# Four graph layers on one core: the set-up in one new order, and layer 1's second filter product ahead of the nodes' products

## The chip, the cores and the metric

The kernel runs on one core of a Trainium2 chip. A core has five engines with a queue of instructions each: TensorE (PE, matrix products, with weight loads counted apart as PEld), VectorE (DVE), ScalarE (ACT), GpSimd (POOL) and SyncE (SP, which here only issues DMAs). ACT and POOL issue DMAs too. Each engine works through its own queue in order. The metric is the device time of one execution in microseconds (us).

## The reference

128 graphs of 64 nodes with 128 channels each, `x [128, 64, 128]`, and `adj [128, 64, 64]`, which is zero for about three quarters of the entries and else a number from 0.05 to 6. Four layers follow one another, each as `x = layernorm(x + layer(x, adj))`. Cut to what matters here:

```python
# layer 0: 20 gaussians of the distance, only edges below 5 count
f = exp(coeff * adj[..., None] ** 2)
rcut = 0.5 * (cos(adj * pi / 5) + 1) * (adj < 5)
W = (ssp(f @ fw1 + fb1) @ fw2 + fb2) * rcut[..., None]
agg = einsum('bjf,bijf->bif', x @ w_in2f, W)
out = ssp(agg @ ow1 + ob1) @ ow2 + ob2
# layer 1: the same with 64 gaussians, and W * adj * adj
g = exp(coeff1 * (adj[..., None] - offsets) ** 2)
Wf = (ssp(g @ W1.T + b1) @ W2.T + b2) * adj[..., None]
y = einsum('bjf,bijf->bif', x @ Wa.T, Wf * adj[..., None])
out = ssp(y @ Wd1.T + bd1) @ Wd2.T + bd2
# layer 2: graph convolutions with the normalised (adj + 1) and elu
# layer 3: relu((normalised (adj + 1) @ x) @ W.T + b)
```

`ssp(v)` is `log(1 + exp(v)) - log 2`. In layers 0 and 1 a filter is computed for every edge: first product (gaussians by W1), exp and log, second product, and then a sum over the neighbours of each node.

## The kernel before

The work is done in `sparse_stack`. (A dense version exists behind a flag and does not run with these inputs.) Two graphs form a pair, so there are 64 pairs with 128 nodes on the 128 partitions.

**Set-up.** Only the edges that exist are computed. To pack them tightly, each graph's nodes are ranked by their number of neighbours, so that nodes with about the same number share a row of slots. The steps, by their names in the code:

- `entries` takes the adjacency, graphs on the partitions, in four quarters. For each quarter DVE writes `within` (below the cutoff) and `some` (not zero).
- `count` adds up each of them over the neighbours, in halving steps. This gives `degree` and `close`. The key of a node is made of both.
- The graphs are sorted by their total (`keys`, `place_on`, `graph_to`); POOL scatters `adj_sorted` and `x_sorted` in that order.
- `rank(0)` ranks the nodes of each graph: four large comparisons `before`, and a count.
- `permuted(0)` permutes the rows of the first eight pairs with PE: 0/1 matrices `there` from DVE, 16 products into `permuted`, a copy to `rows` by ACT, a write to `perm0` and a read back as `ad`. The later eighths go by indirect DMAs on POOL (`scatter`) and loads on SP.
- `compact(0)` takes the nearest neighbours of each row in rounds of eight (`comb`, `at`), and `pack` writes the distances `dc`, the neighbours `jc` and the weight `w` (a Sin on ACT, squared) to DRAM (`store`).
- `loads(n)` reads d, j and w of a pair back, spread over the partitions; in layer 0 the d of one pair comes in six loads.
- `rank(1)` ranks a second time for the later use of the slots, piece by piece. In before, `gathering` runs it, and its pieces lie between those of the compaction.
- A single number of the zero filter (`zero_filter`) is computed by a few small steps of ACT and PE.

The weights of layers 0 and 1 (`filter_layer`) and of layers 2 and 3 are loaded by ACT's queue, all of them ahead of the set-up's first large ACT steps, `below` and `rows`.

**The loop.** It visits 128 pairs, 64 for layer 0 and 64 for layer 1, in three chunks k = 0, 1, 2 each. Three chunks are in flight: c starts, c1 follows, c2 ends.

- `filter_in(c)`: the first product `px` (line 1774), then `h` = exp on ACT. `gather(c1)`: the features of the neighbours by a 0/1 matrix `hot`, product `pg` (line 1800), copied to `g` by ACT. `softplus(c)`: the log on ACT.
- `filter_out(c2)`: the second product `pw` (line 1788). `message(c2)`: DVE's `m` = (pw + bias) * g (line 1814). After a pair's third chunk `slot_sums` reduces m into `agg` in DVE steps that lie in the queue `sums`.
- Work on nodes lies in further queues of generators, of which each slot of the loop runs one step: `befores` (transposing x and multiplying with the input weights), `nodes` (the products after the sum, and the layernorm), `convs` (layer 2 and 3), and `last` for the last small groups. Where a step ends with a product, `owing` lets the step that reads it come one slot later. A full group is four pairs.

`px`, `pg` and `pw` have one PSUM buffer each (two banks), the node products two (`ps_n`).

**The order.** `in_order` chains the instructions of an engine as they are written. In before it does so for DVE and POOL in the set-up, and for all five engines from the loop on; PE, ACT and SP are placed by the scheduler in the set-up, so that a load that waits for nothing may go out earlier than where it is written.

Of the kernel before, what the change touches and what calls it, by code (L numbers as in the profile page):

```python
# [12 lines left out]
F32 = mybir.dt.float32  # L13
# [588 lines left out]
def sparse_stack(ctx: ExitStack, tc: tile.TileContext, t: dict, out: bass.AP, flag):  # L602
# [122 lines left out]

    def load_matrix(name, rows=C):
        w = const.tile([rows, C], F32, name=f"w_{name}")
        nc.scalar.dma_start(w, t[name])
        return w
# [4 lines left out]
    def load_column(name):  # L734
        b = const.tile([P, 1], F32, name=f"c_{name}")
        nc.scalar.dma_start(b, column(name))
        return b
# [19 lines left out]
    def load_rows(name):  # L757
        b = const.tile([P, C], F32, name=f"b_{name}")
        nc.scalar.dma_start(b, dram_ap(t[name], 0, [[0, P], [1, C]]))
        return b  # L760
# [18 lines left out]


# [96 lines left out]
    with (  # L877
        tc.tile_pool(name="count", bufs=2) as pre,
        tc.tile_pool(name="count_ps", bufs=1, space=PSUM) as ps_pre,
    ):  # L880
        entries = pre.tile([NB, A, A], F32, name="entries", bufs=1)
        some = pre.tile([NB, A, A], BF16, name="some", bufs=1)
        within = pre.tile([NB, A, A], BF16, name="within", bufs=1)
        for q in range(4):
            cut = slice(16 * q, 16 * (q + 1))
            nc.sync.dma_start(entries[:, cut, :], adj[:, cut, :])
            nc.vector.tensor_scalar(within[:, cut, :], entries[:, cut, :], CUTOFF, None, ALU.is_lt)
            nc.vector.tensor_scalar(some[:, cut, :], entries[:, cut, :], 0.0, None, ALU.is_gt)

        for into, at in x_parts:  # L890
            nc.sync.dma_start(into, x_flat[:, at])

        degree, close = given[:, 0, :], given[:, 1, :]
        run(deque([count(some, pre, degree), count(within, pre, close)]), -1)
        nc.vector.scalar_tensor_tensor(close, close, -float(A), degree, ALU.add, ALU.add)

        total = const.tile([NB, 1], F32, name="total")
        nc.vector.tensor_reduce(total, given[:, 0:2, :], AX.XY, ALU.add)
        nc.vector.tensor_scalar(total, total, key_of[:, 0:1], key_of[:, 1:2], ALU.mult, ALU.add)
        keys = pre.tile([P, P], F32, name="keys", bufs=1)  # L900
        nc.vector.tensor_scalar(keys, ident, total, None, ALU.mult)
        keys_ps = ps_pre.tile([P, P], F32, name="keys_ps")
        nc.tensor.matmul(keys_ps, lhsT=all_ones, rhs=keys, start=True, stop=True)
        ranking = deque([rank(0, close, pre)])
        run(ranking, 16)
        nc.vector.tensor_scalar(keys, keys_ps, total, None, ALU.is_gt)
        nc.vector.tensor_reduce(total, keys, AX.X, ALU.add)
        nc.vector.tensor_scalar(place_on, columns, total, None, ALU.is_equal)
        to = const.tile([NB, 1], U32, name="graph_to")
        nc.vector.tensor_copy(to, total)  # L910
        nc.gpsimd.indirect_dma_start(
            out=adj_sorted.rearrange("g i j -> g (i j)"),
            out_offset=bass.IndirectOffsetOnAxis(ap=to, axis=0),
            in_=entries.rearrange("g i j -> g (i j)"), in_offset=None,
        )
        run(ranking, -1)
        nc.vector.tensor_mul(width0, width0, width0)
        nc.vector.reciprocal(coeff0, width0)
        nc.vector.tensor_scalar(coeff0, coeff0, -0.5, None, ALU.mult)
        nc.vector.tensor_scalar(neg_off[0], neg_off[0], -1.0, None, ALU.mult)  # L920

        below = pre.tile([NB, A * A], BF16, name="below", bufs=1)
        nc.scalar.activation(
            below, entries.rearrange("g i j -> g (i j)"), AF.Relu, scale=-1.0, accum_out=odd[:, 0:1]
        )

    work = ctx.enter_context(tc.tile_pool(name="swork", bufs=2))
    node = ctx.enter_context(tc.tile_pool(name="snode", bufs=2))
    ps_x = ctx.enter_context(tc.tile_pool(name="sps_x", bufs=1, space=PSUM))
    ps_g = ctx.enter_context(tc.tile_pool(name="sps_g", bufs=1, space=PSUM))  # L930
    ps_w = ctx.enter_context(tc.tile_pool(name="sps_w", bufs=1, space=PSUM))


    compacting = ctx.enter_context(ExitStack())
    cpt = compacting.enter_context(tc.tile_pool(name="scompact", bufs=1))
# [18 lines left out]


# [15 lines left out]

    def goes_to(i):
        if i == 0:
            sorted_ = ps_n.tile([P, 512], F32, tag="n", name="sorted")[:, 0 : 3 * A]
            nc.tensor.matmul(
                sorted_, lhsT=place_on, rhs=given.rearrange("g k i -> g (k i)"),
                start=True, stop=True,
            )
        from_ = sorted_[:, 2 * A :] if i == 0 else places[1]
        nc.vector.tensor_scalar(codes[i], from_, row[:, 2:3], None, ALU.add)  # L980
        tp = ps_n.tile([P, 512], F32, tag="n", name=f"goes_t{i}")
        nc.tensor.transpose(tp[0:A, 0:P], rows_on if i else codes[0], ident)
        by_pair = tp[0:A, 0:P].rearrange("i (p b) -> i p b", b=2)
        for b in range(2):
            to = slice(b * A, (b + 1) * A)
            nc.vector.tensor_copy(a_all[to, :, A] if i else index[to, :], by_pair[:, :, b])

        code = const.tile([P, A], BF16, name=f"code_b{i}")
        nc.vector.tensor_copy(code, codes[i])
        nc.sync.dma_start(code_dram[i], code)  # L990
        if i == 0:
            nc.vector.tensor_copy(table.rearrange("g k i -> g (k i)"), sorted_[:, 0 : 2 * A])

    def find_rows():

        tp = ps_n.tile([P, 512], F32, tag="n", name="graphs")
        nc.tensor.matmul(tp[:, 0:P], lhsT=row_wide, rhs=place_on, start=True, stop=True)
        by_pair = tp[:, 0:P].rearrange("i (p b) -> i p b", b=2)
        row_f = spare[:, 5 * P : 5 * P + NP]
        for b in range(2):  # L1000
            half_ = slice(b * A, (b + 1) * A)
            nc.vector.tensor_scalar(
                row_f[half_], by_pair[half_, :, b], float(A), near[half_], ALU.mult, ALU.add
            )
        nc.vector.tensor_copy(at_row, row_f)


# [27 lines left out]
    def permuted(s, again=False):  # L1035
# [18 lines left out]
        if s == 0 and not again:  # L1054
            goes_first()
            flat = ps_x.tile([P, 2, 512], F32, tag="x", name="permuted0")[:, 0, :]
# [11 lines left out]
            )  # L1068
            for h, engine in enumerate((nc.sync, nc.scalar)):
                from_ = perm0.rearrange("k (q h r) j -> h (k q) r j", h=2, r=8)[h]  # L1070
                engine.dma_start(ad[64 * h : 64 * (h + 1), :, 0:A], from_)
        permuted_rows[s] = ad
        yield

# [5 lines left out]
    def pack(layer, s, d, j):  # L1080
# [28 lines left out]
        for r in range(8):  # L1109
            to = slice(bases[r], bases[r] + caps[r])  # L1110
            nc.gpsimd.tensor_copy(jc[:, to], j[:, r, 0 : caps[r]])
        store("j", jc)
        w = packed("w", F32)
        if layer == 0:
            def sine():
                act(w, dc, AF.Sin, bias=half_pi, scale=PI / (2 * CUTOFF))

            if s == 0:
                sine()
            else:  # L1120
                yield from wait_steps(6)
                sines.append(sine)
                while sines:
                    yield
            yield from wait_steps(PACE if s else 0)
            (nc.gpsimd if s else nc.vector).tensor_tensor(w, w, w, ALU.mult)
# [3 lines left out]
        stored.add((layer, s))  # L1130
        yield
# [148 lines left out]
    def loads(n, engine=nc.sync):  # L1280
        yield_, late = later_loads(n, engine)
        late()
        return yield_

    def later_loads(n, engine=nc.sync):
# [11 lines left out]
        def load(to, name, first, n):  # L1297

            (engine if name == "d" else nc.sync).dma_start(to, dram_ap(slots[layer, name][s], first, [[0, to.shape[0]], [1, n]]))  # L1299
# [3 lines left out]
        for b in range(2):  # L1303
            rows, first = slice(A * b, A * (b + 1)), at + b * size
            if layer == 1:
                load(d[rows], "d", first, size)
            else:
                for k, end in enumerate((NG0, 2 * NG0, A)):
                    load(d[A * b + NG0 * k : A * b + end], "d", first + k * third, third)

        def late():
            for b in range(2):
# [6 lines left out]

    def load_a(s):  # L1320

        a_pairs = (adj_sorted if s else adj).rearrange("(p b) i j -> (b i) p j", b=2)
        nc.sync.dma_start(a_all[:, part(s), 0:A], a_pairs[:, part(s), :])
# [10 lines left out]
    load_a(0)  # L1334
    nc.sync.dma_start(x_all[:, part(0), :], x_pairs[:, part(0), :])
    permuted_rows, goes, hots = {}, {}, {}
    side, again0, sines = deque(), [], deque()

    off1 = offsets1()
# [695 lines left out]
```

## Time and profile before

| | us |
|---|---|
| median of three runs | 1592.23 (1591.06 to 1595.87) |
| the profiled execution | 1607.39 |
| its span | 1605.5 |
| PE busy | 1432.6 |
| DVE busy | 1355.6 |
| ACT busy | 1335.6 |
| POOL busy | 732.5 |

The profile shows one execution, by a hardware profiler; "busy" is the time in which an engine worked on instructions. Its own time is 15.2 us above the median of the runs, so differences are better read from it than levels. The page's slices (40 of equal length) show PE busy under 80% in the first four and the last two, and at 90% or more in all between. The first product of the loop starts at 75.25 us; layer 0 ends and layer 1 starts about in the middle of the span, at 850 us layer 1 is under way, and from some 1540 us on only the last groups' node work is left.

### The profile page before, as it was taken

To read this page: it belongs to the slowest core of one execution; us is meant where nothing else is said; L and a number is where in the kernel's file an instruction comes from. 1 tells how busy PE (TensorE), PEld (TensorE's weight loads), DVE (VectorE), ACT (ScalarE), POOL (GpSimd) and SP (SyncE) were. 2 spreads that over 40 slices of the span, in tenths; PEclk is the share of its full clock that TensorE was granted. 3 is DMA by queue.
4 is the path that set the end of the run, shared out by engine and by line. 5 is a ranking of instruction groups with operands and counts; after the bars stand their busy time and mean duration, and the time that the engine had idled before them with its cause. 6 is when DMAs were issued, how large, how long until landed. Compare 5 with 4: busy or idle time off the path is not lost.

```text
span 1605.5 us, 24221 instructions
## 1 busy us (share of the span) xinstructions
PE 1432.6 (89%) x6813; PEld 802.6 (50%) x6813; DVE 1355.6 (84%) x3547; ACT 1335.6 (83%) x1847; POOL 732.5 (46%) x1174
## 2 busy tenths in 40 slices
PE   1276999999999999999999999999999999999974
PEld 1133454555554555555445555556555555555543
DVE  7687889999989999889878888888888888888873
ACT  1266898989888989889999998999989999899842
POOL 2425246555655644425611255433554435543454
PEclk9998999999999999999999999999999999999976
DMA  7654464645455544447555455544554455455200
GB/s 257 209 123 114 112 138 123 135 124 145 124 136 134 136 122 113 113 111 178 149 151 129 128 142 132 129 124 125 144 132 120 120 134 138 124 141 123 64 8 23
DMA packets 122289, 205.67 MB, mean 128 GB/s; under 512 B 47956, under 2 KB 80034, under 8 KB 121506
## 3 DMA queue, kind: packets, MB, share of 16 engines
q1 hardware_dynamic: 110784, 187.61, 46.7%
q0 software_dynamic: 6576, 14.99, 2.9%
q10 hardware_dynamic: 4786, 1.43, 0.4%
q8 instruction: 57, 0.93, 0.3%
q14 instruction: 86, 0.70, 0.2%
HBM read 185.29 MB, written 18.64 MB: 127 GB/s over the span
## 4 chain that ended last, share of the span: by engine, by line
PE 45%; DVE 27%; ACT 10%; DMA 7%; issue 6%; SPq 3%; POOL 2%; another core or an unknown queue 1%; ACTq 0%; DVEq 0%; POOLq 0%
PE pw L1788 16%; PE px L1774 9%; DVE m L1814 8%; PE pg L1800 7%; DVE agg L1837 6%; ACT h L951 4%; DVE hot L1762 2%; DVE at L1182 2%; PE hw L1673 2%; SPq L1299 2%; ACT g L951 2%; PE y L1453 2%; ACT d L951 1%; DVE st L1415 1%; PE o L1584 1%
## 5 line engine op out<-in xcount | busy, mean ns | idle before, releaser
L951 ACT ACTIVATE h<-h,half 128x672 f32<-128x672 f32 (+13 forms) x385 | 353.1, 917 | 0.1
L1837 DVE TENSOR_REDUCE agg<-m 128x16 f32<-128x240 f32 (+13 forms) x896 | 325.0, 411 | 3.0
L951 ACT ACTIVATE g<-pg 128x672 f32<-128x672 f32 (+12 forms) x384 | 303.2, 790 | 26.4 <-DVE m L1814 13.2
L1800 PE MATMUL pg<-hot,ys 64*128 64x336 f32 (+12 forms) x1536 | 308.8, 478 | 7.9 <-DVE hot L1762 7.0
L1788 PE MATMUL pw<-h,w_L_gnn_W2T 128*128 128x420 f32 (+5 forms) x768 | 301.9, 516 | 15.2 <-DVE m L1814 15.2
L1814 DVE SCALAR_TENSOR_TENSOR m<-pw,c_L_gnn_b,g 128x840 f32<-128x840 f32 (+5 forms) x192 | 200.9, 1046 | 115.6 <-PE pw L1788 88.0
L1788 PE MATMUL pw<-h,w_L_gnn_fw 128*128 128x336 f32 (+6 forms) x768 | 264.4, 467 | 28.3 <-DVE m L1814 22.0
L951 ACT ACTIVATE h<-px,c_L_gnn_b 128x840 f32<-128x840 f32 (+5 forms) x192 | 178.7, 931 | 53.6 <-PE px L1774 52.8
L1814 DVE SCALAR_TENSOR_TENSOR m<-pw,c_L_gnn_fb,g 128x672 f32<-128x672 f32 (+6 forms) x192 | 176.9, 921 | 50.0 <-PE pw L1788 31.2
L951 ACT ACTIVATE h<-px,c_L_gnn_fb 128x672 f32<-128x672 f32 (+6 forms) x192 | 159.3, 830 | 71.2 <-PE px L1774 46.4
L1788 PEld LDWEIGHTS pw<-h,w_L_gnn_W2T 128*128 128x128 f32 x768 | 132.5, 191 | 141.1 <-DVE m L1814 37.6
L1774 PE MATMUL px<-d,fw 64*128 64x336 f32 (+6 forms) x768 | 166.2, 507 | 40.8 <-DMA d<-d_dram 29.2
L1800 PEld LDWEIGHTS pg<-hot,ys 64*128 64x128 f32 x1536 | 146.3, 188 | 108.1 <-issue 17.5
L1788 PEld LDWEIGHTS pw<-h,w_L_gnn_fw 128*128 128x128 f32 x768 | 132.5, 191 | 120.6 <-DVE m L1814 62.2
L1762 DVE SCALAR_TENSOR_TENSOR hot<-j,row,w 128x1212 f32<-128x1212 bf16 (+12 forms) x128 | 177.0, 1383 | 9.0 <-issue 9.0
L1774 PE MATMUL px<-d,w1t 64*128 64x420 f32 (+5 forms) x768 | 181.1, 548 | 1.7 <-ACT h L951 1.6
L1422 POOL TENSOR_SCALAR rs<-mv 128x4 f32<-128x4 f32 x61 | 14.5, 237 | 344.0 <-DVE mv L1416 335.6
L1774 PEld LDWEIGHTS px<-d,fw 64*128 64x128 f32 x768 | 59.7, 188 | 132.2 <-ACT h L951 44.4
L951 ACT ACTIVATE d<-d,neg_off 128x1212 f32<-128x1212 f32 (+12 forms) x128 | 119.8, 936 | 7.1 <-issue 7.1
L1428 POOL TENSOR_SCALAR x_all<-ny,mv,rs 128x128 f32<-128x128 f32 x124 | 116.4, 947 | 3.3
L1030 POOL DMA_INDIRECT rows<-comb,goes x64 | 67.9, 1061 | 97.1 <-DMA rows<-comb,goes 69.6
L1774 PEld LDWEIGHTS px<-d,w1t 64*128 64x128 f32 x768 | 57.8, 184 | 66.8 <-ACT g L951 26.8
(264 smaller groups left out, 2209.6 us busy)
## 6 DMA issues: line engine op xcount, KB each, us to landing
d<-d_dram SPq DMA_DIRECT2D x32, 315.0 KB
w<-w_dram SPq DMA_DIRECT2D x32, 315.0 KB
d<-d_dram SPq DMA_DIRECT2D x32, 303.0 KB
w<-w_dram SPq DMA_DIRECT2D x32, 303.0 KB
w<-w_dram SPq DMA_DIRECT2D x32, 252.0 KB
j<-j_dram SPq DMA_DIRECT2D x32, 157.5 KB
j<-j_dram SPq DMA_DIRECT2D x32, 151.5 KB
d<-d_dram SPq DMA_DIRECT2D x16, 300.0 KB
```

The source lines that it names most:

```text
L951: latest = nc.scalar.activation(out_, in_, func, **kw)
L1030: nc.gpsimd.indirect_dma_start(out=into, out_offset=bass.IndirectOffsetOnAxis(ap=at, axis=0), in_=rows, in_offset=None,)
L1182: nc.vector.max_index(out=at[:, r, cut], in_max=top[:, r, cut], in_values=av[:, r, :])
L1299: (engine if name == "d" else nc.sync).dma_start(to, dram_ap(slots[layer, name][s], first, [[0, to.shape[0]], [1, n]]))
L1428: (nc.gpsimd if n == GS else nc.vector).tensor_scalar(dst[:, s, :], y[:, s, :], mv[:, s, 0:1], rstd[:, s : s + 1], ALU.subtract, ALU.mult,)
L1453: nc.tensor.matmul(ps[:, s, :], lhsT=xt[:, s * P : (s + 1) * P], rhs=w["win"], start=True, stop=True)
L1762: nc.vector.scalar_tensor_tensor(hots[n][:, 0:size], j[:, 0:size], near, wt[:, 0:size], ALU.is_equal, ALU.mult)
L1774: nc.tensor.matmul(ps[:, b, 0:n], lhsT=w1, rhs=d[rows, col : col + n], start=True, stop=True)
L1788: nc.tensor.matmul(c["pw"][:, b, :], lhsT=c["w"]["w2"], rhs=c["h"][:, b, :], start=True, stop=True)
L1800: nc.tensor.matmul(ps[:, b, 0:n], lhsT=y[rows, :], rhs=hots[c["n"]][rows, at], start=True, stop=True,)
L1814: nc.vector.scalar_tensor_tensor(messages[n][:, :, at], c["pw"], c["w"]["b2"], c["g"], ALU.add, ALU.mult)
L1837: nc.vector.tensor_reduce(av[:, :, :, r], both, AX.X, ALU.add)
```

## The change

The set-up is laid out anew, and one place of the loop changes for layer 1.

- The loads of weights go through `queue[0]`. Layer 0's are issued by ACT, ahead of everything else; those of layers 1, 2 and 3 (19 loads) by SP, written behind the first half of `permuted(0)`, the graph sort and the scatters.
- The rank by neighbours below the cutoff comes first. `within` is now made of two instructions per quarter, (below the cutoff) and then (above zero) times that. `count(within)`, `rank(0)` and the products of `permuted(0)` stand ahead of `some`, `count(some)` and the graph sort. `below` is written ahead of the copy `rows`.
- `in_order` now chains all five engines from the beginning to the end.
- In `pack`, Sin stands ahead of j's store in the first eighth, the square of w goes to POOL, and the loads of the first two pairs are issued inside it. Four of the first pair's six d loads are issued by ACT, two by SP.
- `rank(1)` is run at a written place: 17 of its steps ahead of the loop's first loads, the others just ahead of the loop. `gathering` waits 31 steps in its place.
- The loads of x's second part (`load_x(1)`) and of `caps` stand behind the first pairs' slot loads and `permuted(1)`, as they did in the text before, but are now kept there.
- In layer 1 (`n >= NP`) `filter_out(c2)` stands ahead of `last` and `nodes`; `befores` takes its step at k = 0 rather than 1, ahead of `softplus`; the reductions run 2, 4 and 5 at the three chunks rather than 1, 4 and 4. A pause in `node_after` and one of two steps in `graph_convs` are left out, and one is put ahead of the product `o3`.

The instructions of layer 0's loop stand in the same order on every engine in both kernels, apart from its first visits.

The diff, cut to its core (moved functions whose text is the same are left out):

```diff
+    queue = [nc.scalar]
...
-        nc.scalar.dma_start(w, t[name])
+        queue[0].dma_start(w, t[name])
...
+    layers = [filter_layer(0)]
+    queue[0] = nc.sync
...
             nc.vector.tensor_scalar(within[:, cut, :], entries[:, cut, :], CUTOFF, None, ALU.is_lt)
-            nc.vector.tensor_scalar(some[:, cut, :], entries[:, cut, :], 0.0, None, ALU.is_gt)
+            nc.vector.scalar_tensor_tensor(
+                within[:, cut, :], entries[:, cut, :], 0.0, within[:, cut, :], ALU.is_gt, ALU.mult
+            )
...
+        load_a(0)
+        nc.sync.dma_start(x_all[:, part(0), :], x_pairs[:, part(0), :])
         for into, at in x_parts:
             nc.sync.dma_start(into, x_flat[:, at])
+        below = pre.tile([NB, A * A], BF16, name="below", bufs=1)
+        act(
+            below, entries.rearrange("g i j -> g (i j)"), AF.Relu, scale=-1.0, accum_out=odd[:, 0:1]
+        )
...
-        run(deque([count(some, pre, degree), count(within, pre, close)]), -1)
-        nc.vector.scalar_tensor_tensor(close, close, -float(A), degree, ALU.add, ALU.add)
+        run(deque([count(within, pre, close), rank(0, close, pre)]), -1)
+        first_rows = permuted(0)
+        next(first_rows)
+
+        for cut in quarters:
+            nc.vector.tensor_scalar(some[:, cut, :], entries[:, cut, :], 0.0, None, ALU.is_gt)
+        run(deque([count(some, pre, degree)]), -1)
...
+        run(deque([first_rows]), -1)
...
+        if layer + s == 0:
+            sine()
         store("j", jc)
...
-            (nc.gpsimd if s else nc.vector).tensor_tensor(w, w, w, ALU.mult)
+            nc.gpsimd.tensor_tensor(w, w, w, ALU.mult)
...
         store("w", w)
         stored.add((layer, s))
+        if layer + s == 0:
+            slot_data[0] = loads(0)
+            slot_data[1] = loads(1)
+            yield
...
+                    engine = nc.scalar if n == 0 and b * k == 0 else nc.sync
...
-    layers = [filter_layer(0), filter_layer(1)]
+    layers.append(filter_layer(1))
...
-    run(deque([compact(0)]), -1)
     zero_filter = const.tile([P, 1], F32, name="zero_filter")
     nc.vector.tensor_add(zero_filter, u[:, 0:1], w["b2"])
+    first_slots, ranks = compact(0), deque([rank(1, table[:, 0, :], work)])
+    while 0 not in slot_data:
+        next(first_slots)
+    run(ranks, 17)
...
-        elif q < len(GROUPS[1]) - 1:
-            yield
...
             scaled(2, q)
-            yield from wait_steps(2)
...
         y3 = yield from times("sup", lambda s: xs[:, s, :], lambda s: nT3[:, s, :])
+        if n == GS:
+            yield
...
-        yield from rank(1, table[:, 0, :], work)
+        yield from wait_steps(31)
...
-        run(sums, (1, 4, 4)[k])
+        run(sums, ((1, 4, 4), (2, 4, 5))[n >= NP][k])
...
             gather(c1)
+        if n >= NP and k == 0 and befores:
+            slot(befores)
         if c is not None:
             softplus(c)
...
-        slot(nodes)
-        if k == 1 and befores:
-            slot(befores)
+        if n < NP:
+            slot(nodes)
+            if k == 1 and befores:
+                slot(befores)
+        if c2 is not None:
+            filter_out(c2)
         for queue in last.values():
             slot(queue)
+        if n >= NP:
+            slot(nodes)
         if c2 is not None:
-            filter_out(c2)
             message(c2)
...
-    in_order(before_loop, block[-1], (nc.tensor, nc.scalar, nc.vector, nc.gpsimd, nc.sync))
+    in_order(first, block[-1], (nc.tensor, nc.scalar, nc.vector, nc.gpsimd, nc.sync))
```

## The prediction

> **What bounds the kernel.** I read the page's head and its groups first, then the busy times by window, then the chain of waits of the first 90 us, then single engines around the places that these named.
>
> ```profile
> span 1605.5 us, 24221 instructions
> ## 1 busy us (share of the span) xinstructions
> PE 1432.6 (89%) x6813; PEld 802.6 (50%) x6813; DVE 1355.6 (84%) x3547; ACT 1335.6 (83%) x1847; POOL 732.5 (46%) x1174
> ...
> L1814 DVE SCALAR_TENSOR_TENSOR m<-pw,c_L_gnn_b,g 128x840 f32<-128x840 f32 (+5 forms) x192 | 200.9, 1046 | 115.6 <-PE pw L1788 88.0
> ```
>
> TensorE leads, but 89% is an average of three regimes. In the windows below the columns are length, PE, PEld, DVE, ACT, POOL, granted clock, DMA share, GB/s:
>
> ```profile
> 60.00:80.00 20.00, 3.80 (x12) 1.76 (x12) 6.49 (x37) 6.95 (x9) 13.01 (x24) 1.00 0.51 134
> 200.00:400.00 200.00, 189.18 (x902) 101.52 (x902) 189.18 (x564) 179.18 (x263) 105.16 (x178) 1.00 0.55 133
> 1100.00:1300.00 200.00, 194.16 (x958) 112.64 (x956) 167.96 (x359) 183.51 (x235) 93.80 (x115) 1.00 0.52 129
> 1540.00:1560.00 20.00, 13.44 (x57) 9.79 (x56) 13.75 (x42) 9.52 (x26) 9.01 (x11) 0.66 0.02 7
> ```
>
> Set-up (to about 75) waits on one thing after another; layer 0 has PE and DVE level; layer 1 has PE at 97% with DVE at 84%; the tail after 1540 is latency. The change touches the first, third and fourth.
>
> The chain through the set-up (start, us, what):
>
> ```profile
> 30.27 7.73 DMA w_L_gnn_W<-in_L_gnn_W_dram
> ...
> 39.30 0.60 ACT rows L951
> 40.06 3.48 DMA perm<-rows
> 43.59 3.70 DMA ad<-perm
> 47.39 0.43 DVE same L1172
> ...
> 72.18 2.98 DMA d<-d_dram
> 75.25 1.64 PE px L1774 x4
> ```
>
> A copy of 0.60 us (`rows`) stands behind ACT's weight DMAs: PE had its input (`permuted`) ready at 37.0. The compaction starts at 47.39, ends with `dc` at 63.82, and the first product comes at 75.25.
>
> **Part 1, rank first, weights behind.** The four `within` instructions become eight; the second kind, on 1024 columns, I put at 1.2 us (`hot`, the same operation on 1080 columns, takes 1.34). They end near 12.9. Then by the rows of before: one count 3.3, key 0.3, four comparisons 4.55, count 3.4, bits 1.4, place and eight 0/1 matrices 2.7. That is 28.6; the 16 products (3.65 for them before) end near 31. On ACT the loads ahead of the copy shrink to layer 0's, but one of them still waits for a semaphore that the 3 MB load of x holds (the wait that ended at 22 to 23.4 in before); then 8 issues of some 0.46, the table load 1.28, `below` 3.62: the copy runs near 31.5 instead of 39.30. Write 3.48 and read 3.70: `ad` is there at 39, 8 us earlier.
>
> DVE, now in one written order, isn't free then: `some` 2.7, count 3.3, the graph keys, `goes_t` and its casts, and `zero_filter`, which waits for four small ACT and PE steps. The compaction starts near 42.8: 4.6 us earlier. It no longer carries rank(1)'s pieces (1.75 us between 47 and 63), so `dc` is done at 57.5, **6.3 earlier**. Storing d first, and Sin ahead of j's store, makes the way from `dc` to the first Square 8.2 instead of 10.15: the first product at about 67, **8 earlier**. Rank(1), about 11 us of DVE, then lies under the loads, where DVE idles 9.03 us before `hot` and 7.39 before the first m; the PE wait of 2.32 us for `rows_on` goes with it.
>
> A rule that speaks against the moved loads: the Trainium skill, "DMA: Bandwidth & Descriptors", section "Issuing engines are not separate DMA queues", says that transfers started by different engines end on the same 16 DMA engines, so that another issuer saves only issue time. By it, moving 19 loads from ACT to SP gains nothing of the transfers, and costs SP 19 issues of some 0.45 = 8.6 us. The trace puts the gain elsewhere: ACT's table load ahead of `rows` waited 9.61 us with its queue blocked. By the rule alone this part is worth nothing or less; by the row, up to 8 us. I follow the row: SP has those 8.6 us to spare while `ad` is compacted.
>
> **Part 2, what the order on SP gives back.** In before, the loads of x's second part and the caps were free of any order with respect to the slot loads, and ran at 29 to 59. Now they stand where they are written: behind the slot loads of n=0 and 1 and the 16 loads of the second `ad`, ahead of n=2's d.
>
> ```profile
> 76.64 7.29 SPq L1052 DMA_DIRECT2D ad<-perm  x16
> 83.97 2.76 SPq L1299 DMA_DIRECT2D d<-d_dram  x6
> ```
> ```profile
> 90.51 0.59 ACT L951 ACTIVATE d<-d,neg_off 128x360 f32<-128x360 f32 x1
> ```
>
> Before, n=2's d was asked for by 86.7 and the Square stood at 90.51 without a wait. After: slot loads end near 71, `ad` 7.3, four x loads 2, the caps out, 1.8 until landed, and in again, six d loads 2.8: issue ends at 84.5, and 2 to 3.5 us later (the first d took 2.98) it is there. Square(2), which would stand at 82.3, runs near 87.3; ACT is held some 5 us, and everything behind it (Exp, Ln, the copies g), so PE too. **Of 8 us, 3 last.** Ends: 0 if SP's chain runs 3 us later than I count, 8 if x and the caps issue without waiting (10 with the PE wait for `rows_on`). I take 3.
>
> Here a second rule bears: "TensorE: Matmul & The Clock Gate", section "What's actually happening", has PE at half rate after an idle window of some 3.4 us. In this trace four `px` products took 1.64 us after 29 us of idling and 0.88 when warm, while the granted clock of that window reads 1.00: the row has the effect where the clock column doesn't. By the rule a hold of 5 us at n=2 makes the next wave cold too, 1 to 2 us on top; by the row nearest to it, PE idle 2.32 us, the next four took 0.94, nothing. I take 0 and keep 2 in the range.
>
> **Part 3, layer 1's order.** The loop issues px, pg, node products, pw, and then m on DVE reads pw. Pw has a single buffer, so a pw waits for the m before it. Two pw with only px and pg between are 3.15 us apart, less than DVE needs:
>
> ```profile
> 1126.31 0.94 PE L1774 MATMUL px<-d,w1t 64*128 64x400 f32 x4
> 1127.08 0.84 PE L1800 MATMUL pg<-hot,ys 64*128 64x400 f32 x4
> 1128.92 1.61 PE L1788 MATMUL pw<-h,w_L_gnn_W2T 128*128 128x400 f32 x4 [1.00 <-DVE m L1814]
> ```
>
> In layer 1 (850 to 1500) pw waits for m 25 times, 15.2 us in all (at most 1.1), out of some 17 to 20 us of PE idleness: about 1.0 + 0.3 us in each group of four pairs (some 50 us). The product is now ahead of the node steps, the befores move to k=0, one pause is taken out and one put in. Counting products from the new instruction order, each interval between pw's then holds at least one node product: PE intervals of 3.5 to 4.9 us over a group's twelve chunks. DVE's work between two m's is 2.2 to 4.2 us in nine of the twelve, and 5.0, 5.2 and 3.6 in the others, each after one with slack; by my count m is late by at most 1.25 us, just covered by the slack of the interval. What was waiting 1.3 us a group falls to 0.2: 13 groups give **14 us**. Ends: 7 if half of the waits return at other chunks (m also waits for ACT's `nh`, 11.8 us there, which shows that the margins are thin), 17 if all goes. PE's own work is unchanged (no product added or removed), so nothing beyond its idleness can be won here; the order of layer 0's loop is the same in both kernels.
>
> **Part 4, the tail.** Two node products (`o` of the last full group, `gx` of the next) move ahead of the last pw, and the next group's run a few waves earlier. With waves of some 1 to 1.5 us each that are waits mostly, I take 2 us; ends -3 and +6, since another order of short steps can lose as well.
>
> **Sum.** 3 + 14 + 2 = 19. The profiled execution took 1607.39 us, so 1588 by its measure. The median of before is 15.2 below that; the profile holds stalls without a releaser (10.66 us at 147.41, 2.86 near 98) that no part of the change touches and that make up most of those 15.2. So I take the difference, not the level: 1592.2 - 19 = **1573**.
>
> **The rivals.**
> A, *the whole set-up lead lasts* (0.2): SP's loads turn out early enough. For it: ACT and SP idle for long before 75; against: the 16 `ad` loads alone take 7.29. Then 9 + 14 + 2 gives 1567.
> B, *half the loop gain, nothing of the set-up* (0.2): n=2 takes back all 8, and new chunks wait. For it: DVE busy 84%, 1 us pw waits that move easily. 0 + 7 + 1 gives 1584.
> C, *DVE becomes the bound at k=0* (0.13): in layer 1 that chunk now holds `hot` 1.46, two reductions 0.8, m 1.04 and up to 1.9 of node steps, 5.2 us against a PE interval of 3.5 to 3.9. If the lateness exceeds the interval's slack in most pairs, PE stands 0.5 us in each of 64 pairs: 32 lost, 19 won, 1605. It decides from a lateness of about 0.3 us per pair. Against: DVE has 16% to spare and m's are the only thing that PE waits for; k=0 follows a light chunk.
> D, *the loop order does nothing* (0.07): the waits return in full at other chunks; 3 + 2 gives 1587.
> The main case has 0.4, alone 1568 to 1579.
>
> **Numbers.** A measurement can't tell changes below 0.3%, 4.8 us, from none: faster is below 1587.4, slower above 1597. Main, A and most of B and D are faster: 0.80. Same 0.08, slower 0.12 (C, and a bad tail). The range leaves out the top of C and the bottom of A: 1560 to 1589.
>
> **What would show it.** First px at 67 (right: 65 to 69); ACT's Square of n=2 waiting 3 to 6 us for a d; in layer 1 pw's waits for m below 5 us and PE above 98% in 1100 to 1300. It is wrong if pw still waits over 10 us there, or if DVE's idleness before m vanishes.

## The result, and the profile after

| | before | after | ratio, 95% interval |
|---|---|---|---|
| first measurement, median us | 1592.16 | 1575.34 | 0.9879 (0.9858 to 0.9900) |
| a second one, on another chip | 1595.50 | 1572.38 | 0.9868 (0.9842 to 0.9895) |

The changed kernel is 16.8 us faster by the medians; 19 were forecast, which lies within the interval of the ratio (16 to 23 us). The page of after, its head and the groups of layer 1's second product and its message (busy, mean ns, idle before and its cause), and the second product in before:

```profile
span 1574.4 us, 24209 instructions
## 1 busy us (share of the span) xinstructions
PE 1435.9 (91%) x6813; PEld 812.1 (52%) x6813; DVE 1365.7 (87%) x3549; ACT 1335.9 (85%) x1846; POOL 763.7 (49%) x1175
...
L1805 PE MATMUL pw<-h,w_L_gnn_W2T 128*128 128x420 f32 (+5 forms) x768 | 306.2, 521 | 1.6 <-DVE m L1831 1.6
L1831 DVE SCALAR_TENSOR_TENSOR m<-pw,c_L_gnn_b,g 128x840 f32<-128x840 f32 (+5 forms) x192 | 201.3, 1048 | 104.5 <-PE pw L1805 95.4
```
```profile
L1788 PE MATMUL pw<-h,w_L_gnn_W2T 128*128 128x420 f32 (+5 forms) x768 | 301.9, 516 | 15.2 <-DVE m L1814 15.2
```

The same 6813 products in a shorter span. TensorE's idleness ahead of `pw`, 15.2 us before, is 1.6. But `pw` itself is busy for 306.2 us where it was 301.9.

The spans of the two first profiles differ by 31.1 us, far more than the medians. A second profile of before, unchanged, has a span of 1588.1 and a time of 1589.95, so 17.4 of the 1605.5 us of the first aren't the kernel's. I therefore compare second profiles of both kernels, 1588.1 and 1571.4: 16.7 us apart, as the medians are, though they come from two chips. Where the difference lies is read from the starts of TensorE's products (pairs counted from 0, so that pair 2 is the third):

| at the start of | before | after | after leads by |
|---|---|---|---|
| the first px | 75.89 | 67.46 | 8.4 |
| px of pair 3, chunk 0 | 111.75 | 107.14 | 4.6 |
| px of pair 64 (layer 1 starts) | 728.80 | 725.73 | 3.1 |
| px of pair 76 | 862.30 | 861.59 | 0.7 |
| px of pair 124 | 1461.84 | 1450.61 | 11.2 |
| the last pw | 1520.26 | 1506.81 | 13.5 |
| end | 1588.1 | 1571.4 | 16.7 |

The windows view from pair 76 to pair 124 (columns: length, PE, PEld, DVE, ACT, POOL, clock, DMA share, GB/s), before:

```profile
862.30:1461.84 599.54, 581.14 (x2836) 335.38 (x2841) 501.53 (x1070) 551.54 (x700) 274.53 (x334) 1.00 0.50 130
```

and after:

```profile
861.59:1450.61 589.02, 583.61 (x2842) 341.06 (x2842) 504.50 (x1068) 550.84 (x699) 300.73 (x336) 1.00 0.51 133
```

The same twelve groups of four pairs take 10.5 us less. PE's idleness there falls from 18.4 (599.54 - 581.14) to 5.4, by 13.0; PE's busy time grows by 2.5. So 13 us of idling went, and part came back inside products.

The set-up, as ACT and SP show it (first profiles; start, us, instruction, and in brackets the idle time ahead), ACT before and then both engines after:

```profile
38.01 1.28 ACT L948 ACT_TABLE_LOAD   x1 [9.61 <-DMA w_L_gnn_W<-in_L_gnn_W_dram]
39.30 0.60 ACT L951 ACTIVATE rows<-permuted 128x512 f32<-128x512 f32 x1
```
```profile
30.75 0.60 ACT L933 ACTIVATE rows<-permuted 128x512 f32<-128x512 f32 x1 [1.68 <-PE permuted L1003]
...
90.18 0.59 ACT L933 ACTIVATE d<-d,neg_off 128x360 f32<-128x360 f32 x1 [6.55 <-DMA d<-d_dram]
```
```profile
73.71 7.64 SPq L995 DMA_DIRECT2D ad<-perm  x16
81.40 1.81 SPq L1385 DMA_DIRECT2D x_all<-x_sorted  x4
83.25 0.28 SPq L1895 DMA_DIRECT2D caps_dram<-caps_row  x1
85.56 0.69 SPq L1896 DMA_DIRECT2D caps<-caps_dram  x1
86.30 2.33 SPq L1354 DMA_DIRECT2D d<-d_dram  x6
```

`rows` is copied 8.5 us earlier than before, but the third pair's Square stands at 90.18 against 90.51: SP comes to that d only behind `ad`, x and the caps, and ACT waits 6.55 us for it.

### The profile page after: what moved, and what is told of

Read it like the earlier page. It is cut to its first block, busy times and chain, and to the rows that moved or that the text cites. A ratio compares the mean times of both kernels' runs of the same rounds, so it can differ in the third digit from the quotient of the medians.

```text
span 1574.4 us, 24209 instructions
## 1 busy us (share of the span) xinstructions
PE 1435.9 (91%) x6813; PEld 812.1 (52%) x6813; DVE 1365.7 (87%) x3549; ACT 1335.9 (85%) x1846; POOL 763.7 (49%) x1175
## 4 chain that ended last, share of the span: by engine, by line
PE 33%; DVE 21%; POOL 13%; DMA 10%; ACT 9%; issue 6%; SPq 3%; DVEq 0%; POOLq 0%; ACTq 0%
PE pw L1805 12%; PE px L1791 7%; DVE m L1831 6%; PE pg L1817 5%; DMA out_dram<-gz,at_row 5%; POOL x_all L1441 5%; ACT h L933 4%; DVE agg L1854 4%; DVE hot L1779 2%; POOL rs L1436 2%; SPq L1354 2%; POOL gz L1441 2%; DMA w<-w_dram 2%; ACT g L933 2%; PE hw L1689 1%
## 5 line engine op out<-in xcount | busy, mean ns | idle before, releaser
L933 ACT ACTIVATE g<-pg 128x672 f32<-128x672 f32 (+12 forms) x384 | 303.8, 791 | 28.0 <-DVE m L1831 18.6
L1854 DVE TENSOR_REDUCE agg<-m 128x16 f32<-128x240 f32 (+13 forms) x896 | 319.6, 411 | 2.9
L1805 PE MATMUL pw<-h,w_L_gnn_W2T 128*128 128x420 f32 (+5 forms) x768 | 306.2, 521 | 1.6 <-DVE m L1831 1.6
L1831 DVE SCALAR_TENSOR_TENSOR m<-pw,c_L_gnn_b,g 128x840 f32<-128x840 f32 (+5 forms) x192 | 201.3, 1048 | 104.5 <-PE pw L1805 95.4
L1791 PE MATMUL px<-d,fw 64*128 64x336 f32 (+6 forms) x768 | 165.7, 506 | 28.9 <-ACT d L933 18.8
L1441 POOL TENSOR_SCALAR x_all<-ny,mv,rs 128x128 f32<-128x128 f32 x124 | 105.4, 859 | 3.3
L973 POOL DMA_INDIRECT out_dram<-gz,at_row x56 | 78.6, 1403 | 13.9 <-POOL blocks L1646 4.5
```

Source lines behind the costliest of these rows:

```text
L933: latest = nc.scalar.activation(out_, in_, func, **kw)
L973: nc.gpsimd.indirect_dma_start(out=into, out_offset=bass.IndirectOffsetOnAxis(ap=at, axis=0), in_=rows, in_offset=None,)
L1441: (nc.gpsimd if n == GS else nc.vector).tensor_scalar(dst[:, s, :], y[:, s, :], mv[:, s, 0:1], rstd[:, s : s + 1], ALU.subtract, ALU.mult,)
L1791: nc.tensor.matmul(ps[:, b, 0:n], lhsT=w1, rhs=d[rows, col : col + n], start=True, stop=True)
L1805: nc.tensor.matmul(c["pw"][:, b, :], lhsT=c["w"]["w2"], rhs=c["h"][:, b, :], start=True, stop=True)
L1831: nc.vector.scalar_tensor_tensor(messages[n][:, :, at], c["pw"], c["w"]["b2"], c["g"], ALU.add, ALU.mult)
```

## Experiments

Two theories stood at the start. **Mine**: set-up and loop add up, some 4 us and 12 us; what the first profiles differ by ahead of layer 1 beyond that are stalls of before's profile. **The rival**: the set-up makes the gain, since in the first profiles after leads by 18.6 us where layer 1 begins.

### The two halves, and the first profile of before

The new set-up with the old loop order:

```diff
-        run(sums, ((1, 4, 4), (2, 4, 5))[n >= NP][k])
+        run(sums, (1, 4, 4)[k])
...
-        if n >= NP and k == 0 and befores:
-            slot(befores)
...
-        if c2 is not None:
-            filter_out(c2)
         for queue in last.values():
             slot(queue)
-        if n >= NP:
-            slot(nodes)
         if c2 is not None:
+            filter_out(c2)
             message(c2)
```

with the pauses in the node steps as before. The other half is the same edit turned round, made in the kernel before.

> The new set-up with layer 1's old loop order. Theory (parts add up; most of what the two profiles differ by ahead of layer 1 are stalls without a releaser that only the profiled execution of before holds): 2 to 6 us faster than before, near 1588, and pw's waits for m in layer 1 back at about 15 us. Rival (the 17 to 18 us by which the profile of after leads when layer 1 begins are the set-up's work): about 1575, as fast as the whole change.

> The old set-up with layer 1's new loop order. Theory: 11 to 14 us faster than before, near 1580; pw waits for m under 2 us in layer 1, and sup waits for POOL's x_all some 4 us, as in after. Rival (the set-up makes the gain): within 3 us of before.

Both were measured on a chip where before took 1608.96. The set-up alone: 1603.44, ratio 0.9950 (0.9929 to 0.9971), 5.5 us by the medians and 8.0 by the ratio. The loop alone: 1594.38, ratio 0.9887 (0.9861 to 0.9913), 14.6 and 18.2 us (11 to 14 expected). Neither carries the whole. As expected, pw's waits for m in layer 1 are back at 16.0 us in the first and gone in the second, where `sup` waits 3.1. On that chip the profile of the set-up alone stalls where the first profile of before did; ACT there:

```profile
153.72 0.86 ACT L933 ACTIVATE h<-px,c_L_gnn_fb 128x720 f32<-128x720 f32 x1 [7.93 <-remote]
```

The wait has no releaser that the profile knows. All four profiles taken on that chip (these two and two further on) lose some 11 to 14 us from the second chunk of pair 5 to that of pair 6, the two of after nothing. So before was profiled again, and the set-up measured again:

> The kernel before, unchanged, for a second profile. Theory (the stall of 10.7 us at 147 in its first profile comes with the chip or the execution): where the chip gives before some 1592 to 1596, the profile has no such stall, and its lead over the changed kernel at the first pair of layer 1 is 3 to 7 us in place of 18.6. Rival (the stall is the kernel's own): it stalls again near 147 for over 5 us.

> The new set-up with the old loop order of layer 1, again, for the size of its share. Theory (its lead is cut by the load of the third pair's d, and 4 to 5 us are left): 3 to 7 us faster than before. Rival (the 8 us of the first product last): 7 to 10 us faster.

The second profile of before took 1589.95 and has no such stall: pair 5 to pair 6, second chunk to second chunk, takes 10.7 us (22.0 in the first one). The stall comes with the chip or the execution, not with the kernel; what it is stays open. The set-up alone took 1588.07 against 1592.02, ratio 0.9965 (0.9953 to 0.9977), 4.0 us by the medians and 5.6 by the ratio; its profile leads before by 8.5 us at the first px, 6.6 at pair 3, 5.9 at layer 1's start and 4.1 at the end. That is my theory's size, not the rival's.

The loop alone leads by 12.0 us more at the last pw than at pair 64 (from 7.6 behind to 4.5 ahead): its profile had a set-up 6 us slower than before's own, though not a line of it differs, which I can't explain and don't use.

The changed kernel in the later company:

> The changed kernel itself, on the chip of these runs. Theory (set-up and loop add up): the set-up alone gave 8 us here and the loop alone 18, so 20 to 26 us faster than before, 1583 to 1589. Rival (they share a part of their gain, or the first measurement's 16.8 holds on every chip): 15 to 18 us faster, 1591 to 1594. If the stall of some 8 to 11 us near 145 to 158 belongs to the chip and not to the kernel, this profile has it too.

1572.38 against 1595.50, ratio 0.9868 (0.9842 to 0.9895): 23.1 us by the medians and 21.1 by the ratio (17 to 25). That is within the theory's 20 to 26, but the interval reaches into the rival's 15 to 18, so it doesn't decide. It agrees with the first measurement and, within the intervals, with the sum of the halves (26.2 by the ratios). The run came on another chip than the halves, one where before took 1595.50, so the times that the theory named don't apply; its profile has no stall near 145.

### Which of the loop's edits does it

The place of `filter_out` alone (befores at k=1, reductions 1, 4, 4, all pauses as before):

```diff
         if n >= NP:
             slot(nodes)
+            if k == 1 and befores:
+                slot(befores)
         if c2 is not None:
             message(c2)
```

and the reverse, the new befores, reductions and pauses with `filter_out` in its old place:

```diff
-        if c2 is not None:
-            filter_out(c2)
...
         if c2 is not None:
+            filter_out(c2)
             message(c2)
```

> The changed kernel, with filter_out ahead of the node products as the only one of the loop's edits: befores at k=1, the reductions 1, 4, 4 and the pauses as before. Theory (each interval between two pw needs its node product, and the pauses and befores see to that): about half of the loop's gain stays, 1580 to 1584, with pw waiting for m some 5 to 10 us between 850 and 1500. Rival (the place of filter_out alone does it): within 2 us of the changed kernel, 1573 to 1578.

> The changed kernel with filter_out back behind the node products, the other edits of the loop kept (befores at k=0, reductions 2, 4, 5, the pauses). Theory: some 3 to 8 us slower than the changed kernel, 1578 to 1584, as the balance is half of it. Rival (the place of filter_out alone does it): near the kernel with the old loop, 1586 to 1590.

The place alone: 1602.48, ratio 0.9945 (0.9927 to 0.9964), no better, within the intervals, than the set-up alone measured beside it (0.9950). The other edits alone: 1617.60, ratio 1.0056 (1.0040 to 1.0073), *slower* than the kernel before and 14 us slower than the set-up alone. Both theories and both rivals on these times fell: neither part holds half of the gain, nor does one hold all. (Of the waits, the first theory had 5 to 10 us, and 8.5 came.) From pair 64 to the last pw, in the profiles of this chip and against the set-up alone, the place alone wins 1.9 us and the other edits alone lose 15.4; together (the loop alone) they win 12.6. TensorE's waits between 860 and 1490 (sum, times, longest), first the place alone, then the other edits alone:

```profile
PE pw L1806 <- DVE m L1832: 8.5, 24, 0.5
```
```profile
PE gx L1700 <- POOL x_all L1441: 8.4, 12, 1.5
PE sup L1689 <- POOL x_all L1441: 4.6, 14, 0.9
PE pw L1805 <- DVE m L1831: 4.3, 13, 0.4
```

With the place alone, pw still waits for m in 24 places, each half as long. Intervals without a node product remain: counted from the traces, 35 of the 144 intervals between two pw in the twelve groups hold only px and pg (36 with the set-up alone, none in after), and nearly all of these waits lie there. The twelve groups take 595.81 us against 600.26 with the set-up alone, but the next two pairs lose 4.0 us of that (29.00 against 25.01): PE waits 2.4 us there for GpSimd's `blocks`, and the next products run at about half speed.

With the other edits alone, `gx` comes before pw, and the pause of two slots that stood ahead of it is gone: GpSimd's normalised x isn't there yet in the last four of the twelve groups, and PE stops with pw still to be issued. The waits in sum are not the loss: in the twelve groups PE idles 17.5 us, and 18.8 with the set-up alone. Its busy time is what grows, by 11.2 us (581.44 to 592.65): `sup` and `gx` are stretched by 7 us, as their products wait for x one by one, and px, pg and pw take some 5 us more, in part at half speed behind such waits:

```profile
1335.21 2.67 PE L1805 MATMUL pw<-h,w_L_gnn_W2T 128*128 128x384 f32 x4
```

Such a group of four pw takes 1.56 elsewhere. The first eight groups are 3.7 us faster than with the set-up alone, the last four 13.7 slower. Behind pw, `gx` comes that product later (1.5 us), and in after it waits once, 0.9 us. That the pause and `gx` make this loss is read from the trace; no run puts the pause back by itself, and which of the other edits (befores, reductions, pauses) are needed was not separated.

### The new wait at `sup`

In the profiles of after, `sup` waits as well. Waits of PE between 850 and 1500, second profile of after (in before, `pw` alone waited 15.2 us in 25 places, and `sup` isn't in the list):

```profile
PE sup L1689 <- POOL x_all L1441: 3.8, 11, 0.8
PE gx L1700 <- POOL x_all L1441: 0.9, 1, 0.9
PE pw L1805 <- DVE m L1831: 0.5, 1, 0.5
```

In the twelve groups `sup` also grows from 12.7 us of busy time to 16.4, as its later products wait for their part of x, so it costs 4.0 + 3.7 = 7.7 us. The second profiles, before and after:

```profile
L1673 PE MATMUL sup<-nTs,x_all 128*128 128x128 f32 x96 | 12.7, 275 | 0.0
```
```profile
L1689 PE MATMUL sup<-nTs,x_all 128*128 128x128 f32 x96 | 16.4, 292 | 4.0 <-POOL x_all L1441 3.8
```

GpSimd there (second profile of after):

```profile
1115.60 1.28 POOL L1704 TENSOR_TENSOR x_all<-x_all,b_L_gnn_b 128x512 f32<-128x512 f32 x1
1117.04 1.01 POOL L973 DMA_INDIRECT out_dram<-gz,at_row  x1 [0.16 <-issue]
...
1119.59 3.13 POOL L1441 TENSOR_SCALAR x_all<-gz,mv,rs 128x128 f32<-128x128 f32 x4
```

Ahead of the normalisation that `sup` needs stand the addition of a bias for the *next* group, which came there with `gx`, and a scatter. Two cures: move the addition (the first diff), or move `sup` (the second).

```diff
         y = yield from times("hw1", lambda s: h[:, s, :], lambda s: g["W1"])
+        if n == GS:
+            nc.gpsimd.tensor_tensor(xs, xs, g["b2"].unsqueeze(1).to_broadcast([P, n, C]), ALU.add)
```
```diff
+        if n == GS:
+            yield
         y3 = yield from times("sup", lambda s: xs[:, s, :], lambda s: nT3[:, s, :])
-        if n == GS:
-            yield
```

(In the first, the small groups keep the addition ahead of hw1; the old line behind `gx` is taken out.)

> The changed kernel with GpSimd's addition of the bias of layer 2 to x (1.27 us per group) moved from the step of gx to behind the products hw1. Theory (the products sup wait for GpSimd's x_all, since this addition now lies ahead of it): sup's waits and its stretched products, together some 8 us between 862 and 1452, are gone, and the run is 5 to 9 us faster than the changed kernel. Rival (GpSimd is late for other reasons, its scatters above all, or the wait moves to another product): within 2 us.

> The changed kernel with the products sup one slot later (the pause behind sup put ahead of it). Theory (each interval between two pw needs a node product): sup no longer waits, but one interval of each group holds only px and pg, and pw waits for m there by 0.5 to 1 us: within 4 us of the changed kernel, either side. Rival (only sup's wait counts): 5 to 9 us faster.

The addition later: 1566.15, ratio 0.9824 (0.9798 to 0.9849), 6.2 us below the changed kernel beside it (1563.64 to 1569.57 against 1570.26 to 1579.01). `sup` is back to 13.3 us busy and 0.6 of waiting, and the twelve groups take 582.00 us, 7.0 less than in after. So the wait at `sup` was real and was GpSimd's order. `sup` later: 1573.13, no gain. Its waits go as well, and pw waits for m only 0.5 us, so my reason was wrong: of the 144 intervals 12 are without a node product, as expected, but pw waits in none of them. The twelve groups take 583.66, 5.4 less than in after, but the next two pairs lose 3.7 us of that (29.82 against 26.12), with PE idle for 1.9 ahead of one `nT` and slow products behind it, and the first twelve pairs lose 1.6 (137.49 against 135.86).

### SP's order behind the set-up

All of the third pair's loads ahead of `ad`, x and caps:

```diff
+    slot_data[2] = loads(2)
     run(deque([permuted(1)]), -1)
     run(deque([load_x(1)]), -1)
```

(the loop then leaves them out)

> The changed kernel with all loads of the third pair (d, j, w) issued ahead of the second eighth's 16 loads, x's second part and the caps. Theory (SP's order holds n=2's Square for 6.5 us): the wait is gone, px of the third pair comes 3 to 6 us earlier, and the run is 3 to 6 us faster than the changed kernel. Rival (another load of the same queue, ad of the second eighth or x, is late in its place): within 2 us of the changed kernel.

1576.43, ratio 0.9888 (0.9863 to 0.9913): 4 us slower than the changed kernel beside it by the medians, though the intervals overlap; the 3 to 6 us of gain did not come. ACT's long wait for that d is gone, but DVE, in its one order, has a new one:

```profile
86.78 0.43 DVE L1228 TENSOR_SCALAR same<-ad 128x512 f32<-128x512 f32 x1 [4.70 <-DMA ad<-perm]
```

The second pair's `hot` stands behind it, and its pair 3 starts 2.8 us later than in after. So by this profile `ad` is to stay first, and x and caps are what can move:

```diff
-    run(deque([load_x(1)]), -1)
-    nc.sync.dma_start(caps_dram, caps_row.rearrange("o s i r -> o (s i r)"))
...
             if k == 1 and n + 2 < N:
                 late()
+            if i == 2:
+                run(deque([load_x(1)]), -1)
+                nc.sync.dma_start(caps_dram, caps_row.rearrange("o s i r -> o (s i r)"))
...
```

> The changed kernel with the loads of x's second part and of caps behind the third pair's loads; the second eighth's 16 loads stay ahead. Theory (what stands between in SP's queue costs the lead, and ad is needed first): ACT's Square of the third pair waits 2 to 3 us in place of 6.5 to 7.1, its px comes 2 to 4 us earlier, and the run is 2 to 4 us faster. Rival (n=2's j and w, or the chunk's m, are late then): within 1 us.

> Both edits that should help, the bias addition later and x and caps later. Theory (they lie in different parts of the run and add up): 6 us from the first and 2 to 4 from the second, 8 to 10 us faster than the changed kernel, ratio to before near 0.981. Rival (one takes the other's): no more than 6 us faster than the changed kernel.

x and caps later: in the profile the Square of the third pair stands at 83.94, with a wait of 1.41, and pair 3 starts at 103.61, 3.5 us ahead of after's second profile. The times don't confirm it: 1570.02 against 1592.02, ratio 0.9869 (0.9849 to 0.9888), where the changed kernel has 0.9868 on another chip; a gain of 2 to 4 us is within these intervals. Both edits together: 1563.93 against 1592.02, ratio 0.9828 (0.9811 to 0.9845). That is the lowest median of all, 28 us below before, but no different from the addition alone (0.9824), so the second edit's worth stays unsettled; the first one's does not.

## Why the prediction was right, step by step

- **The set-up's lead, forecast 8 at the first product**: right in size. `rows` at 30.75 (31.5 forecast), the compaction at 42.80 (42.8), first px at 67.89 (67). But the credit that the prediction gives to the weights (by the row of 9.61 us, up to 8) isn't shown: in before `permuted` was ready at 37.0, so that with the weights moved and the rank left in its place `rows` would have come 2.3 us earlier at most. The rest took the earlier rank as well; in after ACT waits 1.68 us for `permuted`. No run moves one without the other. SP's 19 issues took 14.8 us, not 8.6, and ended at 57.5; d was stored at 59.2, 0.5 us behind `dc`, so SP had just enough to spare. (In before, `below` ran at 24.69, between the weight loads; only `rows` stood behind them all.)
- **5 of 8 given back at the third pair, forecast 3 left**: the mechanism is shown by the 6.55 us wait and by the two runs that moved loads. The size was a little off: 4.6 at pair 3. The Square came at 90.18, not 87.3, as the slot loads ended at 73.6 and not 71, and caps' return trip took 2.3 us; that only 0.3 us of Square's lead left 4.6 for the products is because before, too, waited after its Square (for m and px), which my sum had not counted. The same set-up leads by 6.6 there in the profile of the set-up alone, so this number carries some 2 us. Where layer 1 starts, 3.1 are left; the 1.5 us between were not followed up, so that meeting the 3 so closely is luck.
- **No cold clock at the third pair**: wrong as a reading, and the Trainium skill's rule quoted there ("TensorE: Matmul & The Clock Gate", section "What's actually happening") was right in its direction. In the second profile of after PE idles 3.33 us there, and the next products run at about half speed, with a granted clock of 0.83 between 80 and 100:

```profile
90.86 1.57 PE L1791 MATMUL px<-d,fw 64*128 64x360 f32 x4 [3.33 <-ACT h L933]
92.22 1.41 PE L1817 MATMUL pg<-hot,ys 64*128 64x360 f32 x4
93.56 2.77 PE L1805 MATMUL pw<-h,w_L_gnn_fw 128*128 128x360 f32 x4
```

  Warm ones take 0.88, 0.77 and 1.48: 2.6 us lost in these three. The row that I had taken, no slow product behind a gap of 2.32 us, does not hold up. In the second profile of before the pw behind the same gap takes 2.71, and one behind a gap of 1.99 takes 2.68:

```profile
89.24 2.71 PE L1788 MATMUL pw<-h,w_L_gnn_fw 128*128 128x360 f32 x4
101.89 2.68 PE L1788 MATMUL pw<-h,w_L_gnn_fw 128*128 128x360 f32 x4 [1.99 <-DVE m L1814]
```

  The first profile also has a gap of 3.31 us, from 98.35 on, with px at 1.57 and pg at 1.41 behind it, which I passed over. So before loses about 3.3 us here in its second profile, where after loses 2.6: as a difference the forecast of nothing was about right, by luck. And slow products came behind gaps shorter than the 3.4 us of the rule.
- **The loop, forecast 14**: the mechanism was right, and its size is what was off: 10.4 between pair 64 and the last pw. In before 36 of the 144 intervals between two pw in the twelve groups held no node product, and all the waits for m lay in 24 of them; in after there is no such interval. The waits for m fell from 15.2 to 0.5 us between 850 and 1500, more than I said, and PE is busy for 198.84 of the 200 us from 1100 on (first profile). What I had not counted is GpSimd: I checked DVE's and ACT's loads in every new interval, but not when x's normalisation is ready for `sup`, which cost 7.7 us in twelve groups. The added edit that takes it away gives 6.2 us in the times. Smaller terms: pw's own busy time grew by 3.7 us in these groups, but that of `o`, `back` and `u` fell by as much. The first twelve pairs of layer 1 lose 2.4 (133.50 to 135.86): 1.5 of it is busy time, as 16 more products fall into this stretch, and 1.2 a wait of layer 1's first `pg`.
- **The tail, forecast 2**: 3.3 in the second profiles (67.84 to 64.59), about 1 in the first ones, so not sized better than that.
- **The sum**: a loop that gave 3.6 less than forecast was in part made up by a tail that gave 1.3 more, so 16.8 for 19 is not three terms each right.
- **The level**: subtracting the difference from the median, not from the profiled execution, was right; the 31 us by which the first profiles differ would have misled by 14, so the differences of one profile are no safer than its level.
- **The rivals**: A (the whole lead of 8 to 9 lasts) and B (none lasts) are excluded by the second measurement of the set-up alone, whose interval is 3.7 to 7.5 us (the first one, 4.7 to 11.4, excludes B only); C (DVE the bound) did not happen: DVE's idleness ahead of m for pw grew, 88.0 to 95.4; D (the loop does nothing) is excluded by the loop alone.

## What to carry to other kernels

When a product is moved ahead of others, look at every engine that feeds the others, also the lightly loaded one: GpSimd, at 49%, set when `sup` could start, because a short instruction for later work stood ahead of an urgent one. Edits that balance a pipeline belong together: here the place of one product alone was worth nothing measurable in the times, its companions alone cost 14 us, and both gave 12 in the profile of the same chip. And where one written order replaces free placement, list what each queue now holds ahead of the first urgent item.

## What the runs showed of the hardware

Half speed on TensorE followed idle gaps of 3.33 us (the next 5.5 us; 2.77 against 1.48 us for the same four products), but also of 2.37 us in the run of the place alone (px 1.77 against 0.97), of 1.99 us in the second profile of before (pw 2.68), and of 1.88 us in that of `sup` later (px 1.77 against 0.98). A gap of 2.32 us was followed by it in one profile of before (pw 2.71) and not in the other (1.48), so in these runs the length of one gap doesn't tell whether the next products are slow. And one kernel's profile can carry a stall that costs 11 to 14 us near the same place on one chip and none on another (pair 5 to 6: 22.0 and 10.7 us in two profiles of the same kernel), so a difference of two profiles isn't a kernel's gain until a second profile bears it out.
